# A graph-layer kernel whose first 128 source rows are multiplied from a tile kept on chip

## The chip, the core and the metric

The kernel runs on one core of one Trainium2 chip. The metric is the device time in microseconds from the first to the last instruction of the launch, as the median of several runs; a profile of one execution is read beside it. The engines are TensorE (PE in the profile; its weight loads are PEld), VectorE (DVE), ScalarE (ACT), GpSimd (POOL) and SyncE (SP). Transfers between memory and the chip run on 16 DMA engines and are issued from SyncE's, ScalarE's and GpSimd's queues.

## The reference

The kernel computes one residual graph layer on x of shape (8, 4096, 256) with a 4096 x 4096 adjacency matrix:

```python
HW = jnp.einsum('bnf,fo->bno', x, W)
A_norm = relu((adj + adj.T) * 0.5)
D = sum(A_norm, axis=1);  d = D ** -0.5
L_norm = eye(N) - d[:, None] * A_norm * d[None, :]
y = relu(jnp.einsum('nm,bmo->bno', L_norm, HW))
out = layernorm(x + y)
```

The input adjacency is sparse, and unevenly so: an entry (i, j) is present with a chance that falls like one over the root of i times j, so the first rows and columns are nearly full and the last ones nearly empty. Because the matrix is symmetric, row j of A also tells which outputs need source row j.

## The kernel before, in words

**First phase (to about 595 us).** It reads adj in 512 x 512 tiles, adds each to the transpose of its partner, applies the relu, writes the result to memory as `a_dram` and counts the sums of groups of 64 columns in `part`. Beside it, it forms g = d * (x W), 2048 numbers for each of the 4096 nodes (8 batches of 256), and writes it to memory as `g_dram`. The output block of the first 128 nodes ("lead") is multiplied on the way. Both stores have an extra row of zeros at index N = 4096.

**Second phase.** The remaining 31 blocks of 128 output nodes are handled in 16 units: unit u has blocks 2u+1 and 2u+2, and unit 15 has one block alone. `SEQ` gives the order: units 1 to 7, then 0, then 8 to 15. For a unit, every source row j gets a pattern of four bits: which of the unit's four groups of 64 output columns it has an entry in. Rows of a like pattern are put together into lists of 128, each of which becomes one tile, so that a tile's matmul skips the groups that none of its rows needs. The eleven kinds of list stand in `KINDS`; kinds 1, 2, 4 and 8 need one group, 3 and 12 both groups of one block, 5, 10, 9 and 6 one group in each block, and kind 0 takes every row that is left and is multiplied into all four groups. `CAPS` has, for each unit, how many tiles each kind has. It is fixed in the program; rows that find no room lead to a slow path at the end (line 1016) that handles every tile.

The lists are made on the chip, two to four units ahead: `patterns` (line 190) computes the pattern `pat` of every row, `place` and `place_rest` give it a slot, and `index` turns slots into addresses (`gi` into `g_dram`, `ai` into `a_dram`). An unused slot holds the address of the row of zeros.

For each tile, `gather` (line 781) issues two indirect transfers from GpSimd: 128 pieces of rows of A, each 64 or 128 KB in all (line 790, tile `ga`), and 128 rows of g, 1 MB (line 801, tile `g`). Slots that hold the address N are skipped in the second. The g tiles live in a ring of 13 (`RING`), the tiles of A in a pool of 15. GpSimd handles its instructions in order, and the transfers that it issues take turns on eight completion semaphores. The first 13 tiles are gathered ahead of the loop; then, after each step of matmuls, the loop issues as many new gathers as tiles were used.

The order of steps is that of `steps_of` (line 741): the one-group tiles come in pairs (1 with 2, 4 with 8), so that two matmuls of 64 columns can run side by side, and the kind-0 tiles are mixed in between the first pairs. For each step line 990 multiplies the tile into the accumulators of the blocks, four matmuls of 512 columns for each block; each shows as two records in the profile. When a block is complete, ScalarE evicts it (line 677), and VectorE adds the residual, takes the moments and normalises (lines 688 to 725); SyncE's queue writes it out. Every unit thus also moves 2 MB of x in and 2 MB of output out.

The last output block is finished in four parts on several engines (`finish_last`).

Of the kernel before, what the change touches and what calls it, by code (L numbers as in the profile page):

```python
# [9 lines left out]
F32 = mybir.dt.float32  # L10
# [23 lines left out]

SEQ = [1, 2, 3, 4, 5, 6, 7, 0, *range(8, 16)]

CAPS = [
# [16 lines left out]
]  # L54

# [2 lines left out]
def kernel(  # L58
# [25 lines left out]
    nc = tc.nc  # L84
    B, N, F = x.shape
    FO = w.shape[1]
    P = 128
# [5 lines left out]
    G = B * FO  # L93
# [1 line left out]
    Q = 64  # L95
    QU = 4
    HOLD = 10
    RING = 13
    EPS = 1e-5
    NK = len(KINDS)  # L100
    tiles = [sum(caps) for caps in CAPS]
    first = [[sum(caps[:k]) for k in range(NK)] for caps in CAPS]
    mid = KINDS.index(4), KINDS.index(5)
    tmax = max(tiles)
# [16 lines left out]
    a_dram = dram.tile([N + 1, N], F32, name="a_dram")  # L121
    g_dram = dram.tile([N + 1, G], F32, name="g_dram")
# [37 lines left out]
    for k in range(NK):  # L160
        nc.gpsimd.memset(kinds[:, k : k + 1], float(KINDS[k] or -1))
        for u in range(NU):
            nc.gpsimd.memset(limit[:, u, k : k + 1], float(CAPS[u][k] * P))
            nc.gpsimd.memset(base[:, u, k : k + 1], float(first[u][k] * P + 1))
# [8 lines left out]
    def blocks(u):  # L173

        return min(2, NB - 1 - 2 * u)
# [14 lines left out]
    def patterns(u):  # L190

        used = ipool.tile([P, QU, NB], F32, tag="used", name=f"used_{u}", bufs=1)
        nb = blocks(u)
        if nb == 1:
            nc.vector.memset(used, 0.0)
        lo = (2 * u + 1) * 2
        nc.vector.tensor_scalar(
            used[:, : 2 * nb],
            part[:, :, lo : lo + 2 * nb].rearrange("p m s -> p s m"),
            0.0,  # L200
            None,
            ALU.is_gt,
        )
        diag = used[:, :, 2 * u + 1 : 2 * u + 1 + nb]
        nc.vector.tensor_tensor(diag, diag, own[:, :, :nb], ALU.max)
        two = ipool.tile([P, 2, NB], F32, tag="two", name=f"two_{u}", bufs=1)
        uv = used.rearrange("p (b h) m -> p b h m", b=2)
        nc.vector.scalar_tensor_tensor(two, uv[:, :, 1], 2.0, uv[:, :, 0], ALU.mult, ALU.add)
        pat = ipool.tile([P, NB], F32, tag="pat", name=f"pat_{u}")
        nc.vector.scalar_tensor_tensor(pat, two[:, 1], 4.0, two[:, 0], ALU.mult, ALU.add)  # L210
        kind = ipool.tile([P, NK, NB], BF16, tag="kind", name=f"kind_{u}")
        nc.vector.tensor_tensor(
            kind,
            pat.unsqueeze(1).to_broadcast([P, NK, NB]),
            kinds.unsqueeze(2).to_broadcast([P, NK, NB]),
            ALU.is_equal,
        )
        plan[u] = pat, kind
# [82 lines left out]
    def place_rest(u, tot, low):  # L301
# [3 lines left out]
        yield  # L305
        room = CAPS[u][KINDS.index(0)] * P
        nc.vector.tensor_scalar(over[:, u : u + 1], incl[:, NB - 1 : NB], float(room), None, ALU.is_gt)
# [83 lines left out]
    with (  # L391
# [213 lines left out]
        for i in range(NS):  # L605
# [37 lines left out]
            if i == 1:  # L643
                for n, u in enumerate(SEQ[:2]):
                    patterns(u)
                    due += [[2 + n, count_place, (u,)], [4 + n, count_place_rest, (u,)]]
                due.sort(key=lambda d: d[0])
            elif i == 2:
                for n, u in enumerate(SEQ[2:4]):
                    patterns(u)  # L650
                    due.append([1 + n, count_place, (u,)])
                due.append([3, count_place_rest, (SEQ[2],)])
            elif i < 5 and i > 2:

                pieces = spread_early(SEQ[i - 3])
                for n in range(5):
                    due.append([1 + n // 2, next, (pieces, None)])
                due.append([4, collect_index, (SEQ[i - 3],)])
# [10 lines left out]
    def residual(i, ypool):  # L669
        xr = ypool.tile([P, B, F], F32, tag="xr", name=f"xr_{i}", bufs=4)  # L670
        ins = nc.scalar.dma_start(xr, x[:, i * P : (i + 1) * P, :].rearrange("b p f -> p b f"))
        return xr, ins.ins
# [57 lines left out]
    def targets(u, kind):  # L730

        if kind == 0:
            kind = 15 if blocks(u) == 2 else 3
        out = []
        for b in range(2):
            h = kind >> 2 * b & 3
            if h:
                out.append((b, {1: slice(0, Q), 2: slice(Q, P), 3: slice(0, P)}[h]))
        return out

    def steps_of(u):

        of = {k: list(range(f, f + c)) for k, f, c in zip(KINDS, first[u], CAPS[u])}
        groups = []
        for one, two in ((1, 2), (0, None), (3, None), (6, None), (9, None), (5, 10), (12, None), (4, 8)):
            a, b = of[one], of.get(two, [])
            groups.append(
                [[(k, ts[n]) for k, ts in ((one, a), (two, b)) if n < len(ts)] for n in range(max(len(a), len(b)))]
            )

        few, all_rows = groups[:2]
        mixed = [s for n in range(max(len(few), len(all_rows))) for s in few[n : n + 1] + all_rows[n : n + 1]]
        return mixed + list(chain.from_iterable(groups[2:]))

    with (
        tc.tile_pool(name="ypool", bufs=2) as ypool,
        tc.tile_pool(name="rows", bufs=RING + 2) as apool,
        ExitStack() as gath,
    ):
        ring = [  # L760
            gath.enter_context(tc.tile_pool(name=f"gath_{k}", bufs=1)).tile([P, G], F32, name=f"g{k}")
            for k in range(RING)
        ]
        lpool = gath.enter_context(tc.tile_pool(name="spread", bufs=1))
        stat = gath.enter_context(tc.tile_pool(name="stat", bufs=3))
        steps = [(u, step) for u in SEQ for step in steps_of(u)]
        order = [(u, k, t) for u, step in steps for k, t in step]
        got = {}
# [7 lines left out]
        def queue(engine):  # L776

            traced = reversed(nc.cur_bb.bb.instructions)
            return tc.issue_after(next(i for i in traced if i.engine == engines[engine]))

        def gather(n):

            if n >= len(order):
                return
            u, kind, t = order[n]
            gi, ai = plan[u]
            both = len(targets(u, kind)) == 2
            at = apool.tile([P, 2 * P], F32, tag="a", name=f"ga_{u}_{t}")
            with queue("pool"):
                nc.gpsimd.indirect_dma_start(  # L790
                    out=at if both else at[:, :P],
                    out_offset=None,
                    in_=a_pairs if both else a_rows,
                    in_offset=bass.IndirectOffsetOnAxis(ap=ai[:, t : t + 1], axis=0),
                    element_offset=P if both else 0,
                )


            gt = ring[n % RING]
            with queue("pool"):  # L800
                nc.gpsimd.indirect_dma_start(  # L801
                    out=gt,
                    out_offset=None,
                    in_=g_dram,
                    in_offset=bass.IndirectOffsetOnAxis(ap=gi[:, t : t + 1], axis=0),
                    bounds_check=N if n < RING else N - 1,
                    oob_is_err=False,
                )
            got[u, t] = (at, gt)
# [13 lines left out]
        xr = {}  # L823
        for n in range(RING):
            gather(n)
        n = RING
        py = {0: lead}
# [125 lines left out]
        for q, (u, step) in enumerate(steps):  # L953
# [30 lines left out]
            for c in range(G // S):  # L984
                for (b, rows, at, gt), new_rows in zip(work, fresh):
                    both = any(len(targets(u, k)) == 2 for k, t in step)
# [11 lines left out]
            for k, t in step:  # L998
                gather(n)
                n += 1  # L1000
# [15 lines left out]
    with tc.If(short > 0):  # L1016
        with (
# [4 lines left out]
            for i in range(NB):  # L1022
# [5 lines left out]
                for m in range(NB):  # L1028
                    gt = full.tile([P, G], F32, tag="g", name=f"gf_{i}_{m}", bufs=4)
# [10 lines left out]
                z, _ = residual(i, ypool)  # L1040
# [30 lines left out]
```

## Time and profile before

| what | value |
| --- | --- |
| time, median of 3 runs | 1545.31 us (1545.08 to 1547.41) |
| profiled span | 1550.9 us |
| first matmul of a unit to the last one | 595.3 to 1536.1 us |
| gathers of g, from the first start to the last | 279, from 582.9 to 1517.7 us |
| bytes moved | 573.95 MB, 370 GB/s in the mean |
| of these, by GpSimd's queue | 314.40 MB |

The first lines of the page give the busy time of each engine as a share of the whole span, and then how it runs over time. In the time view below each digit is the busy share, in tenths, of one fortieth of the span (38.8 us). The first fifteen digits are the first phase.

```profile
PE   5999989898979988999999999999999999887984
DVE  4676588888464540446667868767057899875543
POOL 3002010011312227666666666766667666665653
DMA  9999999999879889999999999999999999999994
```

A reader should keep in mind that a digit of 9 stands for any share of 90% or more, and that busy engines can still be waiting for each other at a fine grain.

### The profile page before, as it was taken

The page shows a single profiled execution, that of the slowest core. Times are in us where ns is not written, and L with a number is a line of the kernel's source. Part 1 is how long each engine was busy: PE and PEld are TensorE (multiplying, and loading weights), DVE is VectorE, ACT ScalarE, POOL GpSimd, SP SyncE. Part 2 cuts the span into 40 slices and gives each one's busy share as a digit, 9 for nine tenths or more (in the row PEclk, how much of TensorE's full clock was granted, in tenths as well). Part 3 has the DMA queues.
Part 4 walks back from the last instruction along what each step waited for, and adds up shares of the span by engine and source line. Part 5 has one row for each costly group of instructions (what it writes and reads, how often), then busy time and mean ns, then how long its engine had stood idle before and what let it go on. Part 6 is the DMA issues. An engine that isn't in the chain of part 4 may idle for free.

```text
span 1550.9 us, 19311 instructions
## 1 busy us (share of the span) xinstructions
PE 1440.7 (93%) x6416; PEld 762.1 (49%) x6416; DVE 984.7 (63%) x3002; ACT 370.3 (24%) x462; POOL 702.4 (45%) x1063
## 2 busy tenths in 40 slices
PE   5999989898979988999999999999999999887984
PEld 5777877677858753333333333333333333332331
DVE  4676588888464540446667868767057899875543
ACT  3555554444535440010100110110011001100111
POOL 3002010011312227666666666766667666665653
PEclk9999999999989999999999999999999999999997
DMA  9999999999879889999999999999999999999994
GB/s 341 366 357 403 395 383 348 379 339 382 338 257 360 335 340 366 419 365 417 370 384 393 391 416 372 404 407 389 389 358 397 391 392 395 383 375 374 356 392 184
DMA packets 218105, 573.95 MB, mean 370 GB/s; under 512 B 16811, under 2 KB 105179, under 8 KB 180347
## 3 DMA queue, kind: packets, MB, share of 16 engines
q0 software_dynamic: 55616, 314.40, 51.1%
q1 hardware_dynamic: 90352, 123.74, 23.0%
q10 hardware_dynamic: 72032, 134.51, 22.9%
q8 instruction: 53, 0.87, 0.2%
q14 instruction: 52, 0.43, 0.1%
HBM read 453.90 MB, written 136.34 MB: 381 GB/s over the span
## 4 chain that ended last, share of the span: by engine, by line
PE 64%; DMA 18%; DVE 8%; issue 5%; ACT 2%; POOL 2%; another core or an unknown queue 0%; POOLq 0%; ACTq 0%; DVEq 0%; SPq 0%
PE py L990 44%; DMA g<-g_dram,gi 12%; PE pg L526 8%; PE lead L484 5%; DMA a_dram<-sym 3%; PE tr L417 3%; DVE sym L421 3%; PE xtr L515 3%; DVE part L426 2%; DMA xin<-in_x_dram 2%; ACT sym L425 1%; DMA adj<-in_adj_dram 1%; PE lists L352 1%; ACT xt L516 0%; POOL ga L790 0%
## 5 line engine op out<-in xcount | busy, mean ns | idle before, releaser
L990 PE MATMUL py<-g,ga 128*64 128x512 f32 (+1 forms) x3024 | 886.3, 606 | 40.8 <-DMA g<-g_dram,gi 29.6
L990 PEld LDWEIGHTS py<-g,ga 128*64 128x64 f32 (+1 forms) x3024 | 324.6, 153 | 591.2 <-issue 559.2
L801 POOL DMA_INDIRECT g<-g_dram,gi x279 | 314.8, 1128 | 244.9 <-issue 80.9
L790 POOL DMA_INDIRECT ga<-a_dram,ai x279 | 296.8, 1064 | 92.1 <-issue 79.5
L677 ACT ACTIVATE y<-py,minus_r 128x512 f32<-128x512 f32 x120 | 81.1, 687 | 828.7 <-PE py L990 675.1
L688 DVE TENSOR_TENSOR xr<-xr,y 128x2048 f32<-128x2048 f32 x31 | 71.3, 2300 | 282.9 <-ACT y L677 131.6
L526 PE MATMUL pg<-w_sb,xt 128*128 128x256 f32 x1024 | 231.9, 385 | 5.2 <-ACT xt L516 5.2
L421 DVE TENSOR_TENSOR sym<-tr,adj 128x512 f32<-128x512 f32 x256 | 162.7, 682 | 96.9 <-PE tr L417 79.5
L526 PEld LDWEIGHTS pg<-w_sb,xt 128*128 128x128 f32 x1024 | 195.6, 194 | 33.4 <-ACT xt L516 5.6
L426 DVE TENSOR_REDUCE part<-sym 128x32 f32<-128x2048 f32 x64 | 145.4, 2279 | 61.7 <-ACT sym L425 61.7
L417 PE MATMUL tr<-ident,adj 128*128 128x128 f32 x1024 | 138.2, 285 | 31.0 <-DVE sym L421 19.1
L425 ACT ACTIVATE sym<-sym 128x2048 f32<-128x2048 f32 x64 | 122.6, 1916 | 130.2 <-DVE sym L421 117.7
L446 POOL TENSOR_TENSOR r<-e,neg_half 128x4 f32<-128x4 f32 x8 | 8.3, 1040 | 318.3 <-DVE e L445 223.4
L417 PEld LDWEIGHTS tr<-ident,adj 128*128 128x128 f32 x1024 | 118.7, 146 | 60.6 <-DVE sym L421 31.9
L693 DVE BATCH_NORM_STATS2 stats<-xr 128x6 f32<-128x256 f32 x256 | 87.3, 412 | 19.2 <-POOL xr L688 18.1
L515 PE MATMUL xtr<-ident,xin 128*128 128x128 f32 x512 | 72.5, 288 | 18.0 <-DVE sym L421 16.9
L717 DVE TENSOR_SCALAR xr<-xr,mv,root 128x256 f32<-128x256 f32 x248 | 83.8, 409 | 0.1
L484 PE MATMUL lead<-gt,strip 128*128 128x512 f32 x176 | 83.0, 598 | 0.0
L516 ACT COPY xt<-xtr 128x512 f32<-128x512 f32 x128 | 68.1, 592 | 47.0 <-PE xtr L515 46.1
L536 ACT ACTIVATE gt<-pg,r 128x512 f32<-128x512 f32 x88 | 60.6, 689 | 74.8 <-PE pg L526 72.2
L515 PEld LDWEIGHTS xtr<-ident,xin 128*128 128x128 f32 x512 | 59.3, 146 | 34.8 <-DVE sym L421 26.9
L331 DVE TENSOR_TENSOR hot<-iota_q,at 128x1024 bf16<-128x1024 f32 x64 | 74.3, 1220 | 2.6 <-DMA a_dram<-sym 2.6
(134 smaller groups left out, 714.0 us busy)
## 6 DMA issues: line engine op xcount, KB each, us to landing
adj<-in_adj_dram SPq DMA_DIRECT2D x64, 1024.0 KB
a_dram<-sym ACTq DMA_DIRECT2D x64, 1024.0 KB
xr<-in_x_dram ACTq DMA_DIRECT2D x32, 1024.0 KB
out_dram<-xr SPq DMA_DIRECT2D x31, 1024.0 KB
xin<-in_x_dram SPq DMA_DIRECT2D x44, 512.0 KB
g_dram<-gt ACTq DMA_DIRECT2D x22, 1024.0 KB
xin<-in_x_dram POOLq DMA_DIRECT2D x20, 512.0 KB
g_dram<-held ACTq DMA_DIRECT2D x10, 1024.0 KB
```

The lines of the kernel that those rows point to most:

```text
L417: ins = nc.tensor.transpose(pt[:, c * P : (c + 1) * P], tji[:, c, a * P : (a + 1) * P], ident)
L421: nc.vector.tensor_add(sym[:, a, :], pt, tij[:, a, :])
L425: nc.scalar.activation(sym, sym, AF.Relu, scale=0.5)
L426: nc.vector.tensor_reduce(part[:, i * A : (i + 1) * A, j * S // Q : (j + 1) * S // Q], sym.rearrange("p a (c q) -> p a c q", q=Q), AX.X, A ...
L484: nc.tensor.matmul(lead[c], lhsT=strip, rhs=g[:, c * S : (c + 1) * S], start=not done, stop=len(done) == NB - 1, skip_group_check=True,)
L515: nc.tensor.transpose(pt[:, k, c, :], xin[b // H][:, b % H + k, c * P : (c + 1) * P], ident)
L526: ins = nc.tensor.matmul(pg[:, k * FO : (k + 1) * FO], lhsT=xt[:, b + k, c, :], rhs=w_sb[:, c, :], start=(c == 0), stop=(c == FC - 1),)
L693: nc.vector.bn_stats(stats[:, b, :], z[:, b, :])
L717: nc.vector.tensor_scalar(z[:, b, :], z[:, b, :], mv[:, b, 0:1], rstd[:, b : b + 1], ALU.subtract, ALU.mult,)
L790: nc.gpsimd.indirect_dma_start(out=at if both else at[:, :P], out_offset=None, in_=a_pairs if both else a_rows, in_offset=bass.IndirectOff ...
L801: nc.gpsimd.indirect_dma_start(out=gt, out_offset=None, in_=g_dram, in_offset=bass.IndirectOffsetOnAxis(ap=gi[:, t : t + 1], axis=0), boun ...
L990: last_product = nc.tensor.matmul(py[2 * u + 1 + b][c][rows, :], lhsT=at[:, off + rows.start : off + rows.stop], rhs=gt[:, c * S : (c + 1) ...
```

## The change

In eleven of the sixteen units (`HUB`: 0, 1, 3, 6 and 8 to 14) the first 128 rows of A are no longer put into lists. Nearly all of these rows have entries in those units. Their part of the product is formed from a tile `hub` that holds the first 128 rows of g: it is loaded once, in unit 1, and stays on chip. In `patterns` the pattern of these rows is set to zero, so that they get no slot. `steps_of` adds one step of kind 0, with the tile number -1, behind the unit's own kind-0 tiles; in most units this is the fourth step. `gather` answers to that number with a plain transfer of 256 columns of the first 128 rows of A, and with `hub` in place of a gathered tile.

`CAPS` is set anew for what is left, one tile less in each of these units: in units 0, 1 and 6 of kind 0, elsewhere with some tiles moved between kinds. The ring gives up one tile for `hub`, and the tiles' places in it are counted by list tiles alone, since hub steps use none.

```diff
+HUB = {0, 1, 3, 6, *range(8, 15)}
 CAPS = [
-    [2, 3, 3, 3, 2, 1, 2, 1, 2, 1, 7],
-    [1, 3, 3, 3, 2, 1, 1, 1, 2, 1, 5],
+    [2, 3, 3, 3, 2, 1, 2, 1, 2, 1, 6],
+    [1, 3, 3, 3, 2, 1, 1, 1, 2, 1, 4],
     [1, 3, 3, 2, 2, 1, 2, 2, 1, 1, 3],
-    [1, 3, 2, 3, 3, 1, 1, 1, 1, 1, 3],
+    [1, 3, 3, 3, 2, 1, 1, 1, 1, 1, 2],
     [1, 3, 3, 2, 2, 2, 1, 1, 1, 1, 2],
     [1, 3, 3, 2, 2, 1, 1, 1, 1, 1, 2],
-    [1, 3, 3, 2, 2, 1, 1, 1, 1, 1, 2],
+    [1, 3, 3, 2, 2, 1, 1, 1, 1, 1, 1],
     [1, 3, 3, 2, 2, 1, 1, 1, 1, 0, 2],
-    [1, 2, 2, 2, 2, 1, 1, 1, 1, 1, 2],
-    [1, 2, 3, 2, 2, 1, 1, 1, 1, 1, 1],
-    [1, 2, 3, 2, 2, 1, 1, 1, 1, 1, 1],
     [1, 1, 2, 2, 2, 1, 1, 1, 2, 1, 1],
     [1, 2, 2, 2, 2, 1, 1, 1, 1, 1, 1],
     [1, 2, 2, 2, 2, 1, 1, 1, 1, 1, 1],
-    [1, 2, 2, 1, 2, 1, 1, 1, 1, 1, 1],
+    [1, 2, 2, 2, 2, 0, 1, 1, 1, 1, 1],
+    [1, 2, 2, 2, 2, 1, 1, 1, 1, 0, 1],
+    [1, 2, 2, 2, 2, 1, 1, 1, 1, 0, 1],
+    [1, 1, 2, 2, 2, 1, 1, 1, 1, 0, 1],
     [0, 4, 4, 0, 0, 0, 0, 0, 0, 0, 1],
 ]
...
-    RING = 13
+    RING = 12
...
+        if u in HUB:
+            nc.vector.memset(pat[:, :1], 0.0)
...
         few, all_rows = groups[:2]
+        all_rows += [[(0, -1)]] * (u in HUB)
...
+        hub = gath.enter_context(tc.tile_pool(name="hub", bufs=1)).tile([P, G], F32, name="g_hub")
+        hub_loads = []
+        ring_tiles = []
...
+            both = len(targets(u, kind)) == 2
+            at = apool.tile([P, 2 * P], F32, tag="a", name=f"ga_{u}_{t % tmax}")
+            if t < 0:
+                if not hub_loads:
+                    with queue("pool"):
+                        hub_loads.append(nc.gpsimd.dma_start(hub, g_dram[:P, :]))
+                with queue("pool"):
+                    nc.gpsimd.dma_start(at, a_dram[:P, (2 * u + 1) * P : (2 * u + 3) * P])
+                got[u, t] = (at, hub)
+                return
             gi, ai = plan[u]
...
+            n = len(ring_tiles)
             gt = ring[n % RING]
+            ring_tiles.append(gt)
```

The rows of `CAPS` stand for units 0 to 15 from top to bottom; as rows of the diff they shift against each other where rows are removed at one place and added at another.

More of the change, by code (lines that the diff above doesn't have):

```diff
@@ L785, in gather @@
             u, kind, t = order[n]
+            both = len(targets(u, kind)) == 2
[8 more added lines that the diff above has]
+                return
             gi, ai = plan[u]
-            both = len(targets(u, kind)) == 2
-            at = apool.tile([P, 2 * P], F32, tag="a", name=f"ga_{u}_{t}")
             with queue("pool"):
```

## The prediction

> **What bounds the kernel now.** I read the page first (busy shares, queues, chain), then a table of busy time by unit, then GpSimd's waits in two stretches, then the matmul groups by shape.
>
> ```profile
> PE 1440.7 (93%) x6416; PEld 762.1 (49%) x6416; DVE 984.7 (63%) x3002; ACT 370.3 (24%) x462; POOL 702.4 (45%) x1063
> q0 software_dynamic: 55616, 314.40, 51.1%
> L801 POOL DMA_INDIRECT g<-g_dram,gi x279 | 314.8, 1128 | 244.9 <-issue 80.9
> ```
>
> TensorE is busy 93%, which looks like the bound. The page cannot say so: this is a mean over the first 595 us (forming A and g) and sixteen units with different limits. The change touches the units alone. I counted the line 990 matmuls in program order, eight records for each block that a tile is multiplied into, to find where each unit begins on TensorE, and asked for the busy time between those moments. Columns: stretch and length, then busy time of PE, PEld, DVE, ACT, POOL, then clock, DMA share and GB/s. The eight rows are units 8 to 15.
>
> ```profile
> 1149.30:1200.40 51.10, 51.10 (x216) 19.39 (x215) 38.59 (x156) 5.66 (x9) 35.70 (x32) 1.00 1.01 399
> 1200.40:1247.20 46.80, 46.80 (x208) 17.03 (x206) 41.72 (x162) 5.39 (x9) 30.07 (x28) 1.00 1.01 383
> 1247.20:1294.00 46.80, 46.80 (x206) 16.97 (x203) 42.85 (x166) 5.75 (x9) 29.43 (x28) 1.00 1.03 395
> 1294.00:1346.10 52.10, 50.06 (x206) 20.57 (x204) 43.58 (x167) 5.14 (x9) 32.34 (x28) 0.97 1.01 389
> 1346.10:1399.70 53.60, 46.92 (x196) 18.42 (x194) 41.89 (x170) 4.56 (x7) 34.20 (x30) 0.97 1.00 373
> 1399.70:1455.00 55.30, 47.41 (x195) 18.71 (x194) 27.38 (x90) 4.71 (x7) 33.87 (x31) 0.94 0.98 362
> 1455.00:1504.20 49.20, 44.48 (x155) 17.38 (x153) 19.98 (x74) 6.85 (x10) 28.44 (x29) 0.97 1.02 399
> 1504.20:1538.00 33.80, 24.25 (x74) 7.46 (x71) 14.79 (x51) 4.15 (x7) 14.04 (x12) 0.90 0.69 257
> ```
>
> The reader is to see that TensorE never rests in units 8 to 10, and rests 2 to 10 us in each of units 11 to 15, 31 us in all, while the DMA share stays at 1. So the end of the kernel is set by transfers. Unit 10 still draws on tiles loaded ahead. GpSimd's waits say the same (us in total, times, longest); first 1190 to 1520, then 1110 to 1190:
>
> ```profile
> POOL g L801 <- DMA g<-g_dram,gi: 37.0, 31, 2.6
> ...
> POOL g L801 <- PE py L990: 24.8, 19, 3.8
> ...
> POOL g L801 <- PE py L990: 9.4, 6, 3.8
> ...
> POOL g L801 <- issue: 6.5, 18, 0.6
> ```
>
> In units 8 and early 9 a gather waits for TensorE to free its ring tile; later it waits for an earlier gather to land. The second wait has a plain cause: GpSimd's transfers signal on eight semaphores in turn, and each waits for the one eight before it, so four pairs (rows of A, rows of g) can be in flight. Setting each gather's start beside the end of the matmuls that read its ring tile before, I find it within 1 us after that end only for some tiles of units 2 to 4, the last at 803.6 us, and of units 8 and 9, the last at 1189.0 us. Everywhere else the tile had long been free, so the 24.8 us put down to TensorE above are mostly an accident of which semaphore moved last, and the transfers set the pace: from 1189.0 to the last gather at 1517.7 us there are 93 of them, 328.7 us, 3.53 us each. The chain of waits in that stretch is gather after gather:
>
> ```profile
> 1430.04 14.48 DMA g<-g_dram,gi
> 1445.26 11.43 DMA g<-g_dram,gi
> 1456.83 14.32 PE py L990 x46
> 1471.20 14.36 DMA g<-g_dram,gi
> ```
>
> **What the Trainium skill says.** "DMA: Bandwidth & Descriptors", section "Anatomy of one DMA — SWDGE (gpsimd) path", says that semaphore waits happen on the issuing sequencer before dispatch. The trace agrees: at 1415.2 us a gather has started, and the next gather of g, held, starts only at 1421.3 us; nothing behind it on GpSimd goes out before. The same page, section "Bandwidth", gives 6.15 us for 1 MB alone. Here several are in flight, and a megabyte of this queue takes less: 51.1% of 1550.9 us over 314.40 MB is 2.52 us. I use that. "TensorE: Matmul & The Clock Gate", Part 3, says that matmuls on different columns of the array run side by side. The trace agrees:
>
> ```profile
> L990 PE MATMUL py<-g,ga 128*64 128x512 f32 x2216 | 527.0, 607 | 31.8 <-DMA g<-g_dram,gi 28.7 <-issue 3.0
> L990 PE MATMUL py<-g,ga 128*128 128x512 f32 x808 | 365.4, 602 | 9.0 <-issue 7.0 <-DMA g<-g_dram,gi 0.9 <-ACT y L677 0.9
> ```
>
> A 128-column record costs 365.4/808 = 0.45 us, a 64-column one 527.0/2216 = 0.24 us, though each lasts 0.6 us. From the starts of successive steps: a pair of 64-column tiles, or a tile of kind 3, 6 or 9, takes 3.5 us; a 64-column tile alone also about 3.5; kind 0 or a pair (5, 10) 7.0; kind 12 4.8.
>
> **The change, part by part.** *Removed:* one list tile in each of the eleven units (279 gathers become 268). Of the first 128 rows of A, 108 to 128 are used in those units (counted from the inputs), so a unit sheds some 120 rows of 8 KB, 0.98 MB, at 2.52 us per MB 2.5 us of transfer. GpSimd sheds one indirect gather, 1.13 us, which is not on the path (45% busy).
>
> *Added:* a plain load of 256 columns of A's first 128 rows in each such unit: it takes the place of a gather of rows of A of the same size or half, so I count nothing for the transfer. Issuing it is not in the trace in this shape; a plain load of 64 KB costs GpSimd 0.55 us, of 512 KB 0.78 us, an indirect one 1.06 us, so it is 0.3 to 0.5 us cheaper. It uses one of the eight semaphores, so behind it three and a half pairs are in flight instead of four for one turn; gathers queue behind it and TensorE would wait for those. The one load of hub, 1 MB in unit 1, equals the tile that unit 1 no longer gathers: zero. Eleven memsets of one column on VectorE (63% busy) and smaller list tables are hidden beside its other work.
>
> *TensorE:* the hub step is a kind-0 step of 7.0 us. In units 0, 1 and 6 a kind-0 tile goes: zero. Unit 3: a single 64-column step gets shorter, -0.9. Unit 8: a kind-0 goes, a kind 9 comes, +3.4. Units 9 and 10: a lone kind 2 goes, +3.4 each. Unit 11: kinds 12 and 9 go, -1.2. Units 12 and 13: kind 6 goes, +3.5 each. Unit 14: +4.3. Sum +19.4 us, nearly all in units 8 to 14, where TensorE rests 31 us with unit 15.
>
> *The ring of 12:* a gather may run ahead by 12 tiles, and hub steps don't count among them. Where transfers are behind, tiles are freed long before: from 1284 us on, the tile 12 back had been free for 12 us or more. It binds only in units 2 to 4, 8 and 9.
>
> Now the path. Units 1 to 5: the gather at 803.6 us waits for the (5, 10) step of unit 3, whose two tiles are freed together; with 12 it waits for the same step. So what unit 3 saves is lost: 0. Unit 6 saves 2.5 us ahead of TensorE's stalls at units 7 and 0 (steps of 8.3, 9.3 and 5.7 us instead of 3.5, 7.1 and 3.5, 9.2 us lost): -2.5 for all that follows. Unit 0 is TensorE's own (107 us, of which it is busy 105.6), so its saving buys nothing: 0. Unit 8 begins at 1149.3 - 2.5 us. The gather of unit 9's kind 6 then waits for unit 8's (5, 10), whose end, with the hub step, comes 4.4 + 7.1 + 3.6 + 7.0 + 3.5 + 3.5 + 3.4 + 3.4 + 7.0 = 42.8 us after the unit's begin; the last such wait before came at 1189.0 - 1149.3 = 39.7 us: +3.1. From there transfers set the pace over 328.7 us less five hubs (units 10 to 14) of 2.5 us: -12.5. TensorE has about 358 us of work from unit 8's begin to the end (the steps of the new lists, summed by the durations above), against 42.8 + 328.7 - 12.5 + 18.4 (last gather to last matmul, as before) = 377 us, so it follows. Sum: -2.5 + 3.1 - 12.5 = -11.9. **1545.3 - 11.9 = 1533.4 us.**
>
> **The rivals.** *A, transfers never idle.* The DMA share is 1.01 even in unit 8, where gathers wait for TensorE; then held gathers are made up, and units 6, 0 and 8 to 14 all count: 9 x 2.5 = 22.5, 1522.8 us. Against it: in unit 8 two tiles wait together. *B, semaphores set the pace, not bytes.* A hub step keeps one of a pair's two turns, so it saves half of 3.53, 1.8 us: -1.8 + 3.1 - 8.8 = -7.5, 1537.8 us. For it: gathers wait for landings 31 times; against it: share 1.0. *C, no difference.* One tile less of reserve (3.5 us) at each of the two changes from TensorE's pace to the transfers', and short stalls around hub steps, eat the saving: about 1544 us. *D, slower.* TensorE's added 3.4 + 3.4 us in units 8 and 9, where it is saturated, lands whole, and fewer gathers in flight save nothing: 1545.3 + 6.8 = 1552.1 us. All 19.4 us would give 1564.7; the 31 us of rest speaks against that.
>
> **How the numbers follow.** My forecast, with what lies within 4 us of it, gets 0.46, A 0.18, B 0.17, C 0.07, D 0.12. The range reaches from just below A, as the price of a megabyte is a mean, to the first part of D's side: 1521 to 1545. Below 1542.2 us lie the forecast, A and B: 0.81 of faster, rounded to 0.80; same 0.08; slower 0.12.
>
> **What would show it.** Right: line 990 has 3048 records and 15 to 25 us more busy time; 268 gathers; queue 0 moves near 305 MB at the same share per MB; the stalls at units 7 and 0 shrink by 2.5 us; unit 8 and 9 take 54 and 50 us; units 11 to 15 together become shorter, with less rest of TensorE. Wrong: the last gathers come at the old time (B, C), or TensorE's rest in units 11 to 15 stays at 31 us while its work grows (D), or the gathers' pace outside hubs rises above 3.53 us.

## The result, and the profile after

The changed kernel took 1528.48 us in the median of 4 runs (1527.65 to 1534.08), the kernel before 1545.19 us (1545.02 to 1547.41) on the same chip: a ratio of 0.9896 with a 95% interval of 0.9871 to 0.9922, 16.7 us faster. The forecast was 1533.4 us: the direction was right, and the gain was larger than the 11.9 us that it worked out. Single executions differ: the profile of the changed kernel is of the longest of its four (1534.08 us), and that of the kernel before is of an execution that was longer than all of those timed here (1552.65 us), so the two profiles lie 18.5 us apart.

The page of the changed kernel first: engines, the queue that the change touches (packets, MB, share of 16 engines), then the groups of gathers and of matmuls.

```profile
span 1532.4 us, 19342 instructions
PE 1445.5 (94%) x6440; PEld 763.0 (50%) x6440; DVE 981.0 (64%) x3013; ACT 371.8 (24%) x462; POOL 692.5 (45%) x1053
...
q0 software_dynamic: 54224, 304.94, 50.1%
...
L1008 PE MATMUL py<-g,ga 128*64 128x512 f32 (+1 forms) x2872 | 814.9, 598 | 14.2 <-DMA g<-g_dram,gi 11.9
...
L819 POOL DMA_INDIRECT g<-g_dram,gi x268 | 308.4, 1151 | 216.8 <-DMA g<-g_dram,gi 78.1
...
L1008 PE MATMUL py<-g_hub,ga 128*128 128x512 f32 x176 | 78.3, 597 | 0.0
```

Line 1008 is the old line 990, and its two groups hold 2872 + 176 = 3048 matmul records, of which the 176 are the eleven hub steps. There are 268 gathers. Queue 0 moves 9.46 MB less, and its packets take 50.1% of 1532.4 us, 767.7 us, where they took 51.1% of 1550.9 us, 792.5 us: 24.8 us less of all 16 engines, and again 2.52 us per MB. TensorE's busy time hardly changed, 1445.5 us instead of 1440.7 us.

The table by unit, counted in the same way as before (stretch and length, then busy time of PE, PEld, DVE, ACT, POOL, then clock, DMA share and GB/s), units 8 to 15:

```profile
1148.30:1202.80 54.50, 54.50 (x222) 20.48 (x221) 39.07 (x158) 6.14 (x10) 34.10 (x31) 1.00 0.95 362
1202.80:1253.10 50.30, 50.30 (x216) 19.02 (x214) 42.02 (x165) 5.55 (x9) 34.77 (x31) 1.00 1.00 390
1253.10:1303.30 50.20, 50.20 (x214) 18.96 (x212) 42.20 (x165) 5.45 (x9) 34.29 (x31) 1.00 1.01 399
1303.30:1350.00 46.70, 46.70 (x206) 17.47 (x204) 38.68 (x150) 5.47 (x9) 31.64 (x27) 1.00 1.01 396
1350.00:1398.80 48.80, 46.80 (x198) 17.59 (x196) 44.27 (x178) 5.55 (x9) 31.70 (x28) 1.00 1.00 384
1398.80:1445.30 46.50, 46.50 (x196) 17.63 (x194) 29.46 (x102) 5.53 (x9) 30.14 (x27) 1.00 1.00 385
1445.30:1490.90 45.60, 45.60 (x154) 16.56 (x152) 20.90 (x77) 5.43 (x9) 27.76 (x26) 1.00 1.03 401
1490.90:1519.00 28.10, 21.89 (x74) 6.88 (x70) 12.31 (x46) 3.51 (x6) 10.01 (x10) 0.94 0.72 255
```

Two things are to be seen. Units 8, 9 and 10 became longer, 54.5, 50.3 and 50.2 us instead of 51.1, 46.8 and 46.8, as TensorE has more to do there. In units 11 to 15 TensorE now rests 8.2 us (2.0 in unit 12 and 6.2 in unit 15) where it rested 31, and these five units take 215.7 us (1303.3 to 1519.0) instead of 244.0 (1294.0 to 1538.0). The DMA share is at 1 from unit 9 to unit 14, as before; in unit 8 it is 0.95, where it was 1.01. What TensorE waited for over units 8 to 15 says the same (us, times, longest; the changed kernel, then the kernel before):

```profile
PE py L1008 <- DMA g<-g_dram,gi: 5.0, 3, 2.5
```
```profile
PE py L990 <- DMA g<-g_dram,gi: 28.3, 14, 4.9
```

So in these units the kernel lost waits for rows of g, not work.

Over the whole time of the gathers, the comparison needs no choice of a place. From the first gather of g to the last matmul (PE, PEld, DVE, ACT and POOL busy, clock, DMA share, GB/s), before and after:

```profile
582.90:1536.70 953.80, 913.03 (x3552) 346.05 (x3550) 598.17 (x2265) 85.93 (x127) 612.73 (x559) 0.98 0.99 384
```
```profile
586.30:1517.80 931.50, 917.34 (x3576) 346.71 (x3574) 594.18 (x2272) 87.30 (x127) 603.00 (x549) 1.00 0.99 383
```

The DMA share is 0.99 and the rate 384 and 383 GB/s. 953.8 us at 384 GB/s are 366 MB, and 9.46 MB less at that rate are 24.6 us; the phase became 22.3 us shorter. That the two come so close is in part luck. A second profile of the changed kernel (e0, below) moves the same bytes at a share of 0.98, and its phase is only 13.9 us shorter than before:

```profile
583.80:1523.70 939.90, 922.27 (x3576) 346.08 (x3574) 597.16 (x2274) 85.20 (x127) 599.05 (x549) 1.00 0.98 380
```

Over all sixteen units, then, transfers are close to the bound, but they do have gaps. The largest is at the end of unit 0, from 1100 to 1150 us (before, the changed kernel, the changed kernel again):

```profile
1100.00:1150.00 50.00, 50.00 (x210) 18.59 (x209) 13.49 (x52) 4.66 (x7) 33.69 (x33) 1.00 0.94 360
1100.00:1150.00 50.00, 50.00 (x213) 18.42 (x212) 14.34 (x56) 5.47 (x8) 30.35 (x31) 1.00 0.87 319
1100.00:1150.00 50.00, 50.00 (x207) 18.72 (x207) 12.08 (x46) 3.44 (x5) 24.40 (x24) 1.00 0.71 249
```

GpSimd's waits in the same stretch, in the same order (us, times, longest):

```profile
POOL g L801 <- PE py L990: 5.7, 5, 2.2
POOL g L819 <- PE py L1008: 12.5, 8, 4.6
POOL g L819 <- PE py L1008: 21.1, 8, 8.0
```

Here TensorE never rests, and gathers wait for it to free their ring tiles: in the changed kernel from 1110.5 us on, before from 1135.3 us on. The DMA engines run partly dry meanwhile. So a part of the bytes saved need not come out as time.

"HBM Reference" of the Trainium skill, section "Specifications (TRN2)", puts a core that streams alone at about 425 GB/s, bounded by its 16 DMA engines; this mix of gathers, residuals and stores stays a tenth below that and is still at a share of 0.99.

### The profile page after: what moved, and what is told of

It is laid out like the page before. It is cut to its first block, busy times and chain, and to the rows that moved or that the text cites. A ratio compares the mean times of both kernels' runs of the same rounds, so it can differ in the third digit from the quotient of the medians.

```text
span 1532.4 us, 19342 instructions
## 1 busy us (share of the span) xinstructions
PE 1445.5 (94%) x6440; PEld 763.0 (50%) x6440; DVE 981.0 (64%) x3013; ACT 371.8 (24%) x462; POOL 692.5 (45%) x1053
## 3 DMA queue, kind: packets, MB, share of 16 engines
q0 software_dynamic: 54224, 304.94, 50.1%
## 4 chain that ended last, share of the span: by engine, by line
PE 61%; DMA 19%; DVE 8%; issue 6%; POOL 3%; ACT 2%; POOLq 0%; ACTq 0%; DVEq 0%; SPq 0%
PE py L1008 41%; DMA g<-g_dram,gi 13%; PE pg L530 8%; PE lead L488 5%; DMA a_dram<-sym 4%; PE tr L421 3%; DVE sym L425 3%; PE xtr L519 3%; DVE part L430 2%; DMA xin<-in_x_dram 1%; POOL g L819 1%; ACT sym L429 1%; DMA adj<-in_adj_dram 1%; POOL ga L806 1%; PE lists L356 1%
## 5 line engine op out<-in xcount | busy, mean ns | idle before, releaser
L1008 PE MATMUL py<-g,ga 128*64 128x512 f32 (+1 forms) x2872 | 814.9, 598 | 14.2 <-DMA g<-g_dram,gi 11.9
L1008 PEld LDWEIGHTS py<-g,ga 128*64 128x64 f32 (+1 forms) x2872 | 292.7, 150 | 522.9 <-issue 494.6
L819 POOL DMA_INDIRECT g<-g_dram,gi x268 | 308.4, 1151 | 216.8 <-DMA g<-g_dram,gi 78.1
L806 POOL DMA_INDIRECT ga<-a_dram,ai x268 | 286.9, 1070 | 107.1 <-issue 70.6
L1008 PE MATMUL py<-g_hub,ga 128*128 128x512 f32 x176 | 78.3, 597 | 0.0
```

Of the source, the lines that this page charges most:

```text
L806: nc.gpsimd.indirect_dma_start(out=at if both else at[:, :P], out_offset=None, in_=a_pairs if both else a_rows, in_offset=bass.IndirectOff ...
L819: nc.gpsimd.indirect_dma_start(out=gt, out_offset=None, in_=g_dram, in_offset=bass.IndirectOffsetOnAxis(ap=gi[:, t : t + 1], axis=0), boun ...
L1008: last_product = nc.tensor.matmul(py[2 * u + 1 + b][c][rows, :], lhsT=at[:, off + rows.start : off + rows.stop], rhs=gt[:, c * S : (c + 1) ...
```

## The experiments

The theory to be tested: transfers set the end, and the gain is that of the bytes no longer moved. The rivals: the eight semaphores' turns set the pace (B); savings made where TensorE is saturated are lost (the forecast's own step); the smaller ring takes part of the gain back. Each kernel was timed beside the kernel before on the same chip, and ratios are to that.

### Which units bring it, and what the ring costs

*e1: hub steps in units 8 to 14 alone. e2: in units 0, 1, 3 and 6 alone. e3: the kernel before with a ring of 12.* In e1 and e2 the other units have the lists of before (their rows of `CAPS` are not shown).

```diff
# e1
-HUB = {0, 1, 3, 6, *range(8, 15)}
+HUB = {*range(8, 15)}
# e2
-HUB = {0, 1, 3, 6, *range(8, 15)}
+HUB = {0, 1, 3, 6}
# e3, against the kernel before
-    RING = 13
+    RING = 12
```

> Hub steps in units 8 to 14 alone; units 0, 1, 3 and 6 have their old lists, and hub is loaded in unit 8 (so 6 of the 7 late units save a gather's bytes). Theory T (the last third is bound by the transfers of g, the first part mostly by TensorE, so the late units make the gain): 13 to 16 us faster than before, about 1530. Theory E (the gain comes from the early units, where fewer gathers remove stalls at units 7 and 0): 2 to 5 us faster, about 1541.

> Hub steps in units 0, 1, 3 and 6 alone; units 8 to 14 have their old lists. Theory T: 1 to 4 us faster than before, about 1543, since units 1, 3 and 0 are TensorE's own and only unit 6 stands before a stall. Theory E: 10 us or more faster, about 1533. If the two parts don't add up to the 16.7 us of the whole change, they share a reserve of loaded tiles.

> The kernel before with a ring of 12 tiles and nothing else. The prediction's reading (the ring binds only in units 2 to 4, 8 and 9, and there two tiles are freed at a time): 0 to 1 us slower, 1545 to 1546. The rival (one tile less of reserve at each change from TensorE's pace to the transfers'): 3.5 to 7 us slower, 1549 to 1552.

Measured: e1 0.9925 (0.9900 to 0.9949), e2 0.9982 (0.9962 to 1.0002), e3 1.0034 (1.0015 to 1.0053). On that chip the kernel before took 1551.3 us, so e1 is 11.6 us faster (7.9 to 15.5), e2 2.8 us (between 0.3 slower and 5.9 faster), and e3 5.3 us slower (2.3 to 8.2): the ring's thirteenth tile is not free. (The pool of A's tiles, two larger than the ring, went from 15 to 14 with it.) As they stand, e1 and e2 fit what the forecast had for these two parts, 9.4 and 2.5 us. But all three have a ring of 12. If it costs as much beside hub steps as it does alone, which no run shows, e3 can be taken off the other two. Queue 0 moves 309.12 MB in e1 and 311.27 MB in e2:

| kernel | MB less than before | times 2.52 us | measured, e3 taken off |
| --- | --- | --- | --- |
| e1, late units | 5.28 | 13.3 us | 11.6 + 5.3 = 16.9 us, give or take 4.8 |
| e2, early units | 3.13 | 7.9 us | 2.8 + 5.3 = 8.1 us, give or take 4.3 |

On this reading the early units' savings are paid in full, although the forecast had counted only unit 6's 2.5 us of them, and unit 0's and unit 3's as lost. Without it they are paid in part: 2.8 us for bytes worth 7.9. The profile of e2 shows gathers held at the end of unit 0 as well (10.7 us of waits for TensorE from 1100 to 1150 us, DMA share 0.88). Whether that is the price of the smaller ring or a loss of what unit 0 saves, these runs do not separate.

### Turns or bytes

*e4: the changed kernel, with the hub's load of A cut in two, so that each hub step takes two turns of the semaphores, as a list tile does, and moves the same bytes.*

```diff
-                with queue("pool"):
-                    nc.gpsimd.dma_start(at, a_dram[:P, (2 * u + 1) * P : (2 * u + 3) * P])
+                for c in range(2):
+                    with queue("pool"):
+                        nc.gpsimd.dma_start(
+                            at[:, c * P : (c + 1) * P],
+                            a_dram[:P, (2 * u + 1 + c) * P : (2 * u + 2 + c) * P],
+                        )
```

> The changed kernel, with the hub step's load of A cut into two of 128 columns, so that a hub step takes two of the eight turns, as a gathered tile does, and moves the same bytes. If bytes set the pace: within 1.5 us of the changed kernel, 1528 to 1530. If the turns of the eight semaphores set it (rival B): each of some nine hub steps loses half of 3.5 us again, about 1544 at most, and 1536 if only the seven late ones count half of that.

*e5: the changed kernel, with the first 128 rows of g loaded anew in each hub step, into a tile of a ring of 13. Lists and TensorE's steps are those of the changed kernel; the bytes are back.*

```diff
-                if not hub_loads:
-                    with queue("pool"):
-                        hub_loads.append(nc.gpsimd.dma_start(hub, g_dram[:P, :]))
...
-                got[u, t] = (at, hub)
+                again = ring[len(ring_tiles) % RING]
+                ring_tiles.append(again)
+                with queue("pool"):
+                    nc.gpsimd.dma_start(again, g_dram[:P, :])
+                got[u, t] = (at, again)
```

> The changed kernel's lists and steps, but every hub step loads the first 128 rows of g anew, 1 MB in one plain transfer, into a tile of the ring (13 tiles again). TensorE's work is that of the changed kernel, the bytes are about those of before. If the bytes kept away make the gain: the gain is gone, 1543 to 1552 where before is 1545. If fewer indirect gathers or the new lists make it: most of it stays, 1530 to 1536.

Measured: e4 0.9856 (0.9819 to 0.9893), no slower than the 0.9896 of the changed kernel on its own chip; e5 1.0015 (1.0001 to 1.0028). Eleven turns more cost nothing that can be seen, and the bytes put back take the whole gain away. Queue 0 of e5 (packets, MB, share of the span of 1548.1 us):

```profile
q0 software_dynamic: 55664, 315.42, 51.3%
```

That is 10.48 MB more than the changed kernel's 304.94, eleven loads in place of one. Rival B falls, and the cause of the gain is shown: the bytes. What they are worth is less than 2.52 us per MB. Against the changed kernel, e5 lost 0.0119 of 1547.4 us, 18.4 us (give or take 4.5), which is 1.8 us per MB; the change itself gained 16.7 us for 9.46 MB, 1.8 us per MB too. In both the ring differs by one tile, so its price may be a part of the gap.

### Does TensorE's added work cost anything

*e6: the changed kernel, with the products of the seven hub steps in units 8 to 14 left out (their part of the sums is missing). All transfers stay; TensorE has 7 x 7.0 = 49 us less to do.*

```diff
         for q, (u, step) in enumerate(steps):
+            skip = step[0][1] < 0 and u > 7
...
-            for c in range(G // S):
+            for c in range(0 if skip else G // S):
```

> The changed kernel without the matmuls of the seven hub steps of units 8 to 14; the product of the first 128 rows is left out there, and 49 us of TensorE's work with it. If transfers still set the end: 0 to 6 us below the changed kernel. If TensorE has become the bound of units 8 to 14, as its rest there (3 us, 31 before, unit 15 taken in) could be read: 20 us or more below.

Measured: 0.9905 (0.9887 to 0.9923), the changed kernel's own 0.9896. TensorE's waits over units 8 to 15 show where the 49 us went:

```profile
PE py L1009 <- DMA g<-g_dram,gi: 37.0, 24, 3.8
```

Most of them became waits for rows of g, 37.0 us instead of 5.0, and the end did not move by anything that the intervals can tell. The work that the change adds to TensorE is hidden, although it leaves TensorE little rest (8.2 us with unit 15 taken in, not the 3 us of the expectation). The trace shows one thing more: the gather that waits for unit 8's step (5, 10) starts at 1178.5 us here and at 1191.5 us in the changed kernel. That gather came 13 us earlier, and the end did not follow.

### More of the same, and a surprise

*e7: hub steps in all sixteen units, and `CAPS` set as small as the rows allow: 255 list tiles instead of 268. e8: the kernel before with such tight lists alone: 270 list tiles instead of 279, nearly the same rows of g.* In e7 the plain load of A for unit 15 has only the columns of its one block.

```diff
# e7, against the changed kernel (two rows of CAPS)
-HUB = {0, 1, 3, 6, *range(8, 15)}
+HUB = {*range(16)}
...
-    [2, 3, 3, 3, 2, 1, 2, 1, 2, 1, 6],
+    [2, 2, 2, 2, 2, 1, 2, 2, 3, 2, 5],
...
-    [0, 4, 4, 0, 0, 0, 0, 0, 0, 0, 1],
+    [0, 3, 3, 0, 0, 0, 0, 0, 0, 0, 2],
# e8, against the kernel before (two rows of CAPS)
-    [2, 3, 3, 3, 2, 1, 2, 1, 2, 1, 7],
+    [2, 2, 2, 2, 2, 1, 2, 2, 3, 2, 6],
...
-    [0, 4, 4, 0, 0, 0, 0, 0, 0, 0, 1],
+    [0, 3, 3, 0, 0, 0, 0, 0, 0, 0, 2],
```

> A version meant to beat both: hub steps in all 16 units, and lists that fit the counted rows as tightly as they can (255 list tiles instead of 268, about 40 us less of TensorE's work than in the changed kernel, 4.8 MB less of g). By the price of bytes (2.5 us per MB): 10 to 14 us below the changed kernel, about 1516. If TensorE's work is what counts: 30 us or more below.

> The kernel before (no hub, ring of 13) with lists that fit the counted rows as tightly as they can: 270 list tiles instead of 279, 59 us less of TensorE's work, 26 of it in units 8 to 15, but the same rows of g, since unused slots move nothing. If bytes set the pace: 0 to 8 us faster than before. If the turns of the eight semaphores do: nine turns of 3.5 us, about 25 faster. If TensorE's work does: 30 or more faster.

Measured: e7 0.9633 (0.9613 to 0.9654), 1489.35 us, which beats both kernels by far more than its expectation; e8 0.9859 (0.9837 to 0.9881), 22 us faster than before with only 1.12 MB less in queue 0, worth 2.8 us. Bytes do not explain e8; the 25 us that its expectation gave to the turns would. Two more kernels took its cause apart.

*e11: e8 with 52 us of TensorE's work put back.* In twelve units, the matmuls of one kind-0 tile are done twice in one or both blocks.

```diff
+        twice = {0: 2, 1: 2, 2: 1, 3: 1, 4: 1, 6: 2, 8: 1, 9: 1, 10: 1, 11: 1, 13: 1, 14: 1}
         for q, (u, step) in enumerate(steps):
+            again = twice.get(u, 0) if step[0] == (0, first[u][KINDS.index(0)]) else 0
...
-                for (b, rows, at, gt), new_rows in zip(work, fresh):
+                for (b, rows, at, gt), new_rows in [*zip(work, fresh), *((wk, False) for wk in work[:again])]:
```

> The kernel before with tight lists (e8_tight_lists), with 52 us of TensorE's work put back: in twelve units the matmuls of one kind-0 tile are done twice in one or both blocks, so that tile's part is counted twice in the sums of those blocks. Transfers are those of e8_tight_lists. If the 22 us that tight lists saved came from fewer gathers and unused slots, this keeps them: 0.986 of the kernel before. If they came from less work of TensorE, they are gone: 1.00.

*e9: the changed kernel, with one more kind-0 tile in each of units 8 to 14, all of its slots unused, and not multiplied* (one of the seven rows of `CAPS` is shown).

```diff
-    [1, 1, 2, 2, 2, 1, 1, 1, 2, 1, 1],
+    [1, 1, 2, 2, 2, 1, 1, 1, 2, 1, 2],
...
+            skip = 7 < u < 15 and step[0] == (0, first[u][KINDS.index(0)] + CAPS[u][KINDS.index(0)] - 1)
...
-            for c in range(G // S):
+            for c in range(0 if skip else G // S):
```

> The changed kernel with one more list tile of kind 0 in each of units 8 to 14. The rows already fit in the tiles that were there, so all 128 slots of the added tile are unused: its transfer of g moves nothing, its transfer of A fetches the row of zeros 128 times, 0.13 MB; no matmul is done with it, so only the transfers differ. If only the bytes count: 7 x 0.13 MB at 2.6 us per MB, 2.4 us slower than the changed kernel, about 1531. If each pair of gathers costs its own time whatever it carries (the pairs come 3.5 us apart), or if an unused slot costs as much as a used one: 7 x 3.5 = 24 us slower, about 1553, as slow as the kernel before. Something between is an unused slot's own price.

*The changed kernel once more, as the measure on that chip.*

> The changed kernel once more, as the measure for the other kernels of this chip: 0.9896 of the kernel before, within the interval of the first time (0.987 to 0.992).

Measured on one chip: e11 0.9859 (0.9835 to 0.9884), the changed kernel 0.9879 (0.9844 to 0.9914), e9 0.9928 (0.9900 to 0.9956). The work put back in e11 costs nothing, so e8's gain is not TensorE's. The seven empty tiles of e9 cost 0.9928 - 0.9879 = 0.0049 of 1552.8 us, 7.6 us (0.6 to 14.6, the two intervals' half-widths added as squares): not the 24 us that a full turn or a full tile each would take, and about 1.1 us a tile, of which its 0.13 MB are 0.33. Queue 0 of e9, in a span of 1544.5 us:

```profile
q0 software_dynamic: 55568, 305.86, 49.9%
```

For e8's nine tiles fewer that is some 10 us (1 to 19) of the 22, the tiles' own bytes taken in. The rest is open. In e8 and e11 the same phase runs at 396 and 390 GB/s instead of 384:

```profile
581.80:1505.30 923.50, 867.76 (x3456) 344.96 (x3454) 594.50 (x2265) 87.27 (x128) 595.50 (x541) 0.98 1.01 396
```

The packets of queue 0 took 51.4% of 1519.4 us in e8, 781.0 us, which is 11.5 us less than before where the bytes explain 2.8, and the DMA share of the phase rose from 0.99 to 1.01: each packet took a little less time, and the engines had fewer gaps. Several causes would fit and were not tried apart: an empty tile takes a place in the ring as a full one does, fuller tiles put more rows behind each place and each turn of the semaphores, or they may keep the 16 DMA engines more evenly busy.

### The ring given back

*e10: the changed kernel with a ring of 13; the pool of A's tiles has 13 instead of 14, as there is no other room.*

```diff
-    RING = 12
+    RING = 13
...
-        tc.tile_pool(name="rows", bufs=RING + 2) as apool,
+        tc.tile_pool(name="rows", bufs=RING) as apool,
```

> The changed kernel with a ring of 13 again; the room comes from the pool of A's tiles, 13 instead of 14. If the ring's tile costs what the kernel before showed when it lost it (5 us), this is 3 to 5 us faster than the changed kernel: about 1524. If the ring matters only where a gather waits for TensorE, and the pool of A's tiles (which hub steps use too) now holds the gathers at the same places, the same as the changed kernel within 2 us.

Measured: 0.9897 (0.9847 to 0.9947), beside 0.9879 for the changed kernel on that chip. No gain is seen, but the interval is 8 us wide on each side, and A's tiles, which hub steps use too, now hold gathers in place of g's: in the group of line 806, which fetches A, the idle time rose from 105.5 to 156.4 us, 62.2 of it put down to TensorE. So whether the ring costs 5 us in the changed kernel, as it does in the kernel before, stays unshown.

## Why the prediction was right, and where its sum was wrong

The forecast of 1533.4 us lies 4.9 us above the measured time, and rival A's 1522.8 us lies 5.7 us below it. The mechanism that both share was right. The sum was not: two of its terms were off, in opposite directions.

- *Transfers set the end, and the price of a megabyte:* right in the main. The engine time per megabyte stayed at 2.52 us, e5 shows bytes to be the cause, and the DMA share over the gathers is 0.98 to 0.99. As time of the kernel, a megabyte was worth 1.8 us.
- *TensorE's added 19.4 us are hidden:* right, shown by e6. The rest of 31 us in units 11 to 15 shrank to 8.2, as the waits for rows of g went. TensorE's busy time there did not grow but fell, from 213.1 to 207.5 us, probably for the reason given in the last point.
- *Units 8 and 9 take 54 and 50 us, and a gather of unit 9 that waits for unit 8's (5, 10) starts 42.8 us after unit 8's begin:* right: 54.5 and 50.3 us, and 43.2 us after the begin in the trace. (By the order of the program this gather is that of kind 3; kind 6 comes right behind it.) The hub's plain load of A takes GpSimd 0.587 us (median of 11), inside the 0.56 to 0.76 that the forecast's saving leaves, and in e4 even a second one cost nothing that can be seen.
- *What units 0, 3, 8 and 9 save is lost, because TensorE sets the pace there:* too strict. The forecast split the path at single moments (the gather at 803.6 us, the one at 1189.0 us) and let only the stretches between count. For units 8 and 9 this is wrong: e6 moved the second gather by 13 us and the end stayed, so the 3.1 us that its delay cost the forecast did not belong in the sum. For unit 0 the profiles side with the forecast in part: there gathers are held and the DMA engines run dry, more so with the change. Rival A, in which transfers never idle, erred the other way: 22.5 us against 16.7.
- *A ring of 12 costs nothing:* wrong for the kernel before by e3, 5.3 us (2.3 to 8.2), between one and two of the tiles of 3.5 us that rival C had put against the saving. Nor does the ring stop binding with unit 9: in the changed kernel gathers of units 10 and 11 are held too, the last one at 1292.0 us. As an estimate, all bytes at their engine time less the ring's price, 23.8 - 5.3, give 18.5 us against the measured 16.7. On this reading the forecast paid too little for the bytes and nothing for the ring, and that these errors cancelled in part is luck. That the ring takes its part in the changed kernel too is not shown; e10 could not confirm it.
- *From the gather at 1189.0 us on, 12.5 us less:* too small. That stretch went from 328.7 us to 309.1 us (1191.5 to 1500.6), 19.6 us less. It moved 382 GB/s before and 385 after, which is 125.6 and 119.0 MB, 6.6 less. Five hubs' rows of g are 4.9 of them. By the trace's queues the others are residuals and stores, of which more had been done ahead of this stretch: here the time that the early units left to the transfers was used.
- *The stalls at units 7 and 0 shrink by 2.5 us:* not seen against the kernel before. They grew from 9.1 to 11.7 us, with 2.2 more in unit 6. But in the profile of before TensorE had lost 9.5 us in unit 1 (below), and so came to these units later, when more had landed. In e5, which has the bytes of before and no such loss, TensorE waits 10.4 us for rows of g from 860 to 1100 us, in the changed kernel 6.9. Against that kernel the waits did shrink, though most of e5's lie ahead of unit 7. The sign was badly chosen: a stall is the difference of two paces, and where it falls changes with either.
- *Line 990 has 15 to 25 us more busy time:* wrong as a sign. It has 814.9 + 78.3 - 886.3 = 6.9 us more. The clock column of before is at 0.94 to 0.97 in units 11 to 14 and at 1.00 in the changed kernel, and a mean record took 606 ns before and 598 after; that this hides the rest of the added steps is likely, but no run shows it alone. "TensorE: Matmul & The Clock Gate" of the Trainium skill, Part 1, says that the clock is halved after an idle window; the trace agrees in that the low clocks stand in the units with rest. A busy time that contains slow matmuls is not the work.

## What to carry to other kernels

When the DMA share stands near one over a whole phase, look for bytes to take away, and take bytes times the measured engine time per megabyte as a price that need not be paid in full; here 23.8 us of that became 16.7. Do not let one held gather decide what counts: held transfers can be made up later, as e6 shows. Look instead for stretches in which the DMA share falls while transfers wait for tiles. Price a lost buffer by running the old kernel with one buffer less; here that was 5 us where none had been counted. Then look for transfers that carry little: filling the lists' tiles better was worth about as much as the change itself, and both together, with hub steps in all units, 57 us.

## What the runs showed of the hardware

In the profile of before, TensorE issued records of one kind-0 step 2.1 us apart in unit 1, with nothing named as the cause (start, us, engine and line, idle time before):

```profile
613.15 0.59 PE L990 MATMUL py<-g,ga 128*128 128x512 f32 x1 [0.79 <-issue]
615.25 0.59 PE L990 MATMUL py<-g,ga 128*128 128x512 f32 x1 [1.51 <-issue]
617.35 1.01 PE L990 MATMUL py<-g,ga 128*128 128x512 f32 x1 [1.51 <-issue]
```

The step took 16.5 us instead of 7.1. It is in the profiles of before, e1, e3 and (in another step) e11, and not in those of the changed kernel, e2 and e4 to e10; the cause is open. By unit 8 at most half of the 9.5 us was left: unit 8 begins 566.4 us after the first gather of g in the kernel before and 562.0 us after it in the changed kernel, which also has bytes saved by then.

The gather of an empty tile cost about 1.1 us of the kernel's time although it moves 0.13 MB, and tight lists raised the rate of the whole phase from 384 to 396 GB/s. Both say that the number of gathers, their unused slots or the ring places that they take count beside the bytes.
